# The search's row of norms moved from ScalarE to GpSimd, one tile ahead

## The chip, the cores and the metric

The kernel runs on one core of a Trainium2 chip. A core has five engines that run their own instruction queues in order and meet through semaphores: TensorE (PE in the profile; PEld is its weight load), VectorE (DVE), ScalarE (ACT), GpSimd (POOL) and SyncE (SP), which here only issues transfers. Matmul results lie in PSUM, everything else on chip in SBUF, and 16 DMA engines move data to and from HBM. The metric is the device time of one execution in microseconds (us); smaller is better.

## The reference

Sixteen images of 64 x 64 tokens with 256 channels, float32, pass through four residual layers. Each layer takes a group norm of its input and adds its result to it:

```python
def encode(x, embeddings):                      # layer 0
    xf = x.reshape(-1, x.shape[-1])
    dis = sum(xf*xf, -1) + sum(embeddings*embeddings, 0) - 2.0 * matmul(xf, embeddings)
    return argmin(dis, -1)
x = x + take(embeddings.T, encode(_gn(x), embeddings))   # 1024 codes
x = x + sigmoid(f g^T) h                        # layer 1: attention along each image row of 64
x = x + sigmoid(x2 . softmax(x0 x1^T)) * gn     # layer 2: 4096 x 4096 softmax from three rows, a gate
x = x + layernorm(linear_attention(gn))         # layer 3: 4 heads of 32
```

The change lies in layer 0, the search for the nearest of 1024 codes for each of 65,536 tokens. Beside it, layer 2 matters: for every image it takes the exponential of a 4096 x 4096 outer product and two sums over it.

## The kernel before

The work of an image is cut into stages, each a Python generator: `stats0` (statistics for the first norm), `stage1` (the search), `layer1`, `rows2` and `stage2` (the softmax), `gate2`, and `stage3`. A list of tasks gives every stage of every image a start and a length in units of one image's turn, and a heap takes the generators' steps in the order of those times (L914 to L944). So, in the steady state, VectorE's queue holds, side by side, the search of image b, layer 1 of image b-1, the exponentials of another image, and so on. A scheduler then puts the instructions into one fixed order per engine, and gives them their buffers; at run time each queue is strictly in order.

**The search, `stage1`.** The tokens come in 8 chunks of 4 tiles of 128 tokens. Per image it is 32 tiles, for 16 images 512. For a chunk, `norm` (L329) makes the normed tokens `xn` and their squares `sq` on ScalarE, TensorE sums the squares with a weight of -1 (`px`, L341), ScalarE copies the row (L346), TensorE turns it (`pxt`, L348), and `norm_rows` (L350) copies it on VectorE into `nx2`, four columns of minus the token's squared norm (L353). `ne2`, made once at the start, holds minus the squared norms of the 1024 codes in every partition. For each tile:

- ScalarE makes `nn` = `ne2` + the tile's column of `nx2` (L382), a 128x1024 float32 tile.
- TensorE makes `pd`, twice the products of tokens and codes, in four matmuls (L387).
- VectorE adds `pd` and `nn` into `nn` and takes the largest element (L393), then finds its index (L398).
- GpSimd gathers the 128 rows of the code book by that index and adds them to the tokens `xc`, with an indirect DMA (L399).

`nn` lies in the buffers with tag `t4`, three in number, which `sq`, layer 1's `fg` (L470) and the rows of layer 2 (L578) use too. When a chunk has gone through, `back` (L358) turns the tokens again on TensorE and stores them for layer 1.

**The exponentials, `stage2`.** Per image 64 steps, 1024 in all: ScalarE makes `ex` from the row `x0b` (L627, 128x2048, with the sum as a by-product), and VectorE multiplies `ex` by the row `x2b` and sums it (L630). Both inputs of L630 lie in SBUF. So do those of `gate2`'s L685.

**What else GpSimd does.** In layer 3, `normalize` multiplies the queries by the inverse of their sums (L738), L784 subtracts their maximum; both are `tensor_tensor` instructions on 128x512 in place. L850 takes a power of 4 columns, L280 and L282 finish a group norm, and L611 reduces over the partitions, for which GpSimd's code is exchanged and put back afterwards.

Of the kernel before, what the change touches and what calls it, by code (L numbers as in the profile page):

```python
# [9 lines left out]
F32 = mybir.dt.float32  # L10
BF16 = mybir.dt.bfloat16
U32 = mybir.dt.uint32
AF = mybir.ActivationFunctionType
ALU = mybir.AluOpType
AX = mybir.AxisListType

P = 128
# [4 lines left out]
CH = 4  # L22
# [5 lines left out]
CODES = 1024  # L28
# [13 lines left out]
def kernel(  # L42
# [7 lines left out]
    nc = tc.nc  # L50
# [8 lines left out]
    s1p = ctx.enter_context(tc.tile_pool(name="s1p", bufs=2))  # L59
# [8 lines left out]
    def bank(name):  # L68
        return ps_m.tile([P, 512], F32, tag="pm", name=name)

    def wide(name):
        return ps_w.tile([P, 1024], F32, tag="pw", name=name)
# [113 lines left out]
    ne2 = const.tile([P, CODES], F32, name="ne2")  # L186
# [60 lines left out]
    for n in range(4):  # L247
        t = const.tile([P, 8], F32, name=f"m8_{n}")
# [4 lines left out]
    def stats_tile(kind, name):  # L253
        return small.tile([P, NK, NCHUNK, 6], F32, tag=f"gn_st{kind}", name=name, bufs=1)

    def chunk_stats(st, xt, ch):
        for k in range(NK):
            nc.vector.bn_stats(st[:, k, ch, :], xt[:, k, :])
# [54 lines left out]
    def stage1(b):  # L313
        tag = f"s1_{b}"
        scale, _, nbias = norm0.pop(b)
        src = xT[b].rearrange("(k p) n -> p k n", p=P)
        tok = x[b].rearrange("(t p) c -> p t c", p=P)
        xt, xc, xn, nx2, pxt = {}, {}, {}, {}, {}

        def load(ch):  # L320
            xt[ch] = xa.tile([P, NK, CW], F32, tag="xa", name=f"xt_{tag}_{ch}")
            nc.sync.dma_start(out=xt[ch], in_=src[:, :, ch * CW : (ch + 1) * CW])

        def tokens(ch):
            xc[ch] = s1p.tile([P, CH, C], F32, tag="xc", name=f"xc_{tag}_{ch}")
            nc.sync.dma_start(out=xc[ch], in_=tok[:, ch * CH : (ch + 1) * CH, :])

        def norm(ch):
            xn[ch] = s1p.tile([P, NK, CW], F32, tag="xn", name=f"xn_{tag}_{ch}")  # L329
            sq = s1p.tile([P, NK, CW], F32, tag="t4", name=f"sq_{tag}_{ch}", bufs=3)  # L330
            for k in range(NK):
                nc.scalar.activation(  # L332
                    xn[ch][:, k, :], xt[ch][:, k, :], AF.Identity, bias=nbias[:, k : k + 1], scale=scale[:, k : k + 1]
                )
                nc.scalar.activation(
                    sq[:, k, :], xt[ch][:, k, :], AF.Square, bias=nbias[:, k : k + 1], scale=scale[:, k : k + 1]
                )
            px = bank(f"px_{tag}_{ch}")
            for t in range(CH):
                for k in range(NK):  # L340
                    nc.tensor.matmul(  # L341
                        px[32 * t : 32 * t + 32, :P], lhsT=neg32, rhs=sq[:, k, t * P : (t + 1) * P],
                        start=(k == 0), stop=(k == NK - 1),
                    )
            xrow = small.tile([P, P], F32, tag="xrow", name=f"xrow_{tag}_{ch}", bufs=1)
            nc.scalar.copy(xrow, px[:, :P])  # L346
            pxt[ch] = bank(f"pxt_{tag}_{ch}")
            nc.tensor.transpose(pxt[ch][:, :P], xrow, ident)  # L348

        def norm_rows(ch):  # L350
            px = pxt.pop(ch)
            nx2[ch] = small.tile([P, CH], F32, tag="x2", name=f"nx2_{tag}_{ch}")
            nc.vector.tensor_copy(nx2[ch], px[:, :P].rearrange("p (t n) -> p t n", n=32)[:, :, 0])  # L353

        st1 = stats_tile(1, f"st1_{tag}")
        x1_d[b] = []

        def back(ch):  # L358
            for k in range(NK):
                pt = bank(f"pt_{tag}_{ch}_{k}")  # L360
                for t in range(CH):
                    nc.tensor.transpose(  # L362
                        pt[:, t * P : (t + 1) * P], xc[ch][:, t, k * P : (k + 1) * P], ident
                    )
                nc.scalar.copy(xt[ch][:, k, :], pt)
            chunk_stats(st1, xt[ch], ch)
            d = dram.tile([P, NK, CW], F32, tag=f"x1_{ch}", name=f"x1_{tag}_{ch}")
            nc.scalar.dma_start(out=d, in_=xt.pop(ch))
            x1_d[b].append(d)

        load(0)
        load(1)
        norm(0)
        norm_rows(0)
        tokens(0)
        yield 4
        for ch in range(NCHUNK):
            for t in range(CH):
                T = ch * CH + t

                nn = s1p.tile([P, CODES], F32, tag="t4", name=f"nn_{tag}_{T}", bufs=3)
                nc.scalar.activation(nn, ne2, AF.Identity, bias=nx2[ch][:, t : t + 1])  # L382
                pd = wide(f"pd_{tag}_{T}")
                for hf in range(2):
                    cols = slice(hf * 512, (hf + 1) * 512)
                    for k in range(NK):
                        nc.tensor.matmul(  # L387
                            pd[:, cols], lhsT=xn[ch][:, k, t * P : (t + 1) * P], rhs=e2[:, k, cols],
                            start=(k == 0), stop=(k == NK - 1),
                        )  # L390

                m8 = m8s[T % 4]
                nc.vector.tensor_tensor_reduce(  # L393
                    out=nn, in0=pd, in1=nn, scale=1.0, scalar=-3.0e38, op0=ALU.add, op1=ALU.max,
                    accum_out=m8[:, 0:1],
                )
                i8 = small.tile([P, 8], U32, tag="i8", name=f"i8_{tag}_{T}", bufs=4)
                nc.vector.max_index(i8, m8, nn)  # L398
                nc.gpsimd.indirect_dma_start(  # L399
                    out=xc[ch][:, t, :], out_offset=None,  # L400
                    in_=emb_rows, in_offset=bass.IndirectOffsetOnAxis(ap=i8[:, 0:1], axis=0),
                    compute_op=ALU.add,
                )
                yield 4
                if t == 1 and ch > 0:
                    back(ch - 1)
                    yield 2
                if t == 2 and ch + 1 < NCHUNK:
                    norm(ch + 1)
                    yield 2  # L410
                if t == 3:
                    if ch + 1 < NCHUNK:
                        norm_rows(ch + 1)
                        tokens(ch + 1)
                    if ch + 2 < NCHUNK:
                        load(ch + 2)
        back(NCHUNK - 1)
        with tc.high_priority(offset=URGENT):
            norm1[b] = gn_finish(st1, "n1", b)
        yield 3  # L420
# [518 lines left out]
    while queue:  # L939
        now, n = heapq.heappop(queue)  # L940
        _, length, gen, total = tasks[n]
# [39 lines left out]
```

## Time and profile before

| | |
|---|---|
| timed executions | 5732.52, 5749.94, 5752.01 us; median 5749.94 |
| profiled execution, span from first to last instruction | 5743.5 us (the page gives no other time for it) |
| granted TensorE clock, mean | 0.953 |
| busy: PE / DVE / ACT / POOL | 5264.6 / 5074.3 / 4498.8 / 1721.5 us |
| the same from 1000 to 5000 us | 3777.0 / 3718.6 / 3306.1 / 1270.9 us of 4000 |

Busy time is the union of an engine's instructions; PE's ends are modelled, so its share is an upper view. A group is named by line, engine, operation, tile written <- tiles read; in the names all digits are left out, so `nn_s` is `nn` of the search, `ex_s` the exponentials, `ne` is `ne2`. The idle time beside a group is put down to the instruction whose semaphore came last.

The first image's search runs alone from 40.8 us, the first L630 starts at 320 us, the last search tile's index is looked for at 5056 us and the last L630 starts at 5584 us.

### The profile page before, as it was taken

How to read it: one execution, taken by the hardware profiler on the slowest of the kernel's cores; microseconds unless marked ns; L12 is line 12 of the kernel's file. 1: busy time of each engine (PE TensorE's matmuls, PEld its weight loads, DVE VectorE, ACT ScalarE, POOL GpSimd, SP SyncE). 2: the span in 40 equal slices, each digit the busy share in tenths (PEclk: the TensorE clock that was granted, in tenths of full speed). 3: DMA queues.
4: the chain of work that ended last, by engine and by line, in shares of the span. 5: the costliest groups of instructions: out<-in, count | busy, mean ns of one | idle time of the engine just before them, and what ended most of it. 6: DMA issues, size and time to landing. Idle time of an engine off the chain costs nothing.

```text
span 5743.5 us, 80122 instructions
## 1 busy us (share of the span) xinstructions
PE 5264.6 (92%) x28975; PEld 3227.5 (56%) x28975; DVE 5074.3 (88%) x7186; ACT 4498.8 (78%) x6514; POOL 1721.5 (30%) x1074
## 2 busy tenths in 40 slices
PE   8978899889999999999999999999999999997888
PEld 3534455545656556565655656565565655664556
DVE  6489799999989999998999999999999999998882
ACT  4478588878878788887978788787888879887873
POOL 3123233223333232322323232332323233311221
PEclk9988999989999999999999999999999999998888
DMA  6453836655665656566475656746566674745543
GB/s 184 133 165 93 263 111 196 198 156 170 212 192 174 228 157 217 168 201 223 149 248 158 216 181 198 233 149 223 174 210 194 188 229 151 227 157 180 198 159 116
DMA packets 521380, 1059.52 MB, mean 184 GB/s; under 512 B 52504, under 2 KB 266392, under 8 KB 512792
## 3 DMA queue, kind: packets, MB, share of 16 engines
q1 hardware_dynamic: 406288, 885.11, 45.5%
q0 software_dynamic: 73728, 67.14, 8.2%
q10 hardware_dynamic: 40968, 102.13, 4.6%
q8 instruction: 230, 3.77, 0.3%
q14 instruction: 166, 1.36, 0.1%
HBM read 751.18 MB, written 303.04 MB: 184 GB/s over the span
## 4 chain that ended last, share of the span: by engine, by line
PE 40%; DVE 16%; ACT 11%; issue 4%; DMA 4%; POOL 4%; SPq 0%; ACTq 0%; POOLq 0%; DVEq 0%
PE pd_s L387 12%; DVE ex_s L630 6%; ACT ex_s L627 5%; PE ph_l L477 3%; PE pxo_s L890 3%; PE pqv_s L764 2%; PE pk_s L747 2%; PE po_l L515 2%; DMA qo_s<-qd_s 2%; PE pxo_s L884 2%; PE pz_s L839 2%; POOL qv_s L784 2%; DVE i_s L398 2%; DVE nn_s L393 1%; PE pvr_s L847 1%
## 5 line engine op out<-in xcount | busy, mean ns | idle before, releaser
L630 DVE CUSTOM_DVE_ANT_0 ex_s<-ex_s,x2b 128x2048 f32<-128x2048 f32 x1024 | 2398.0, 2349 | 65.9 <-ACT ex_s L627 65.8
L627 ACT ACTIVATE ex_s<-x0b,nmax_s,x_r 128x2048 f32<-128x2048 f32 x1024 | 2138.1, 2089 | 42.9 <-DVE num_s L630 34.3
L387 PE MATMUL pd_s<-e,xn_s 128*128 128x512 f32 x4096 | 1989.0, 620 | 44.9 <-DVE m L393 33.6
L399 POOL DMA_INDIRECT xc_s<-in_emb_rows,i_s x512 | 1091.3, 2131 | 1926.7 <-DVE i_s L398 1406.6
L387 PEld LDWEIGHTS pd_s<-e,xn_s 128*128 128x128 f32 x4096 | 752.8, 196 | 810.3 <-issue 697.6
L393 DVE CUSTOM_DVE_ANT_0 nn_s<-pd_s,nn_s 128x1024 f32<-128x1024 f32 x512 | 620.2, 1213 | 157.9 <-PE pd_s L387 87.4
L398 DVE FIND_INDEX8 i_s<-m,nn_s 128x8 uint32<-128x1024 f32 x512 | 623.4, 1218 | 0.0
L382 ACT ACTIVATE nn_s<-ne,nx_s 128x1024 f32<-128x1024 f32 x512 | 582.6, 1144 | 45.2 <-DVE nx_s L353 21.5
L477 PE MATMUL ph_l<-wh_l,xt_l 128*128 128x256 f32 x2048 | 525.5, 393 | 20.8 <-DVE m L393 12.1
L764 PE MATMUL pqv_s<-wqv_s,xk_s 128*128 128x256 f32 x2048 | 488.9, 380 | 0.0
L477 PEld LDWEIGHTS ph_l<-wh_l,xt_l 128*128 128x128 f32 x2048 | 382.3, 194 | 135.9 <-issue 64.1
L764 PEld LDWEIGHTS pqv_s<-wqv_s,xk_s 128*128 128x128 f32 x2048 | 388.8, 191 | 119.9 <-issue 60.2
L784 POOL TENSOR_TENSOR qv_s<-qv_s,qm_s 128x512 f32<-128x512 f32 x128 | 195.3, 1526 | 679.9 <-DVE qm_s L783 492.7
L850 POOL TENSOR_TENSOR lrs_s<-lrs_s,mhalf 128x4 f32<-128x4 f32 x128 | 163.6, 1278 | 678.0 <-ACT lrs_s L849 664.2
L515 PEld LDWEIGHTS po_l<-at_l,h_l 64*128 64x128 f32 x4096 | 260.6, 193 | 61.3 <-issue 29.1
L515 PE MATMUL po_l<-at_l,h_l 64*128 64x64 f32 x4096 | 288.7, 283 | 4.5 <-DVE m L393 2.9
L738 POOL TENSOR_TENSOR qv_s<-qv_s,qd_s 128x512 f32<-128x512 f32 x128 | 203.6, 1590 | 266.5 <-DVE qd_s L737 101.4
L890 PE MATMUL pxo_s<-wctx_s,qo_s 128*128 128x256 f32 x1024 | 272.8, 390 | 0.8 <-DVE qo_s L858 0.8
L895 ACT COPY y_s<-pxo_s 128x512 f32<-128x512 f32 x256 | 149.0, 582 | 153.7 <-PE pxo_s L894 131.7
L747 PE MATMUL pk_s<-xk_s,wk_s 128*128 128x512 f32 x512 | 256.6, 624 | 1.5 <-DMA xk_s<-x_g 1.5
L362 PE MATMUL pt_s<-ident,xc_s 128*128 128x128 f32 x1024 | 161.1, 287 | 101.5 <-DMA xc_s<-in_emb_rows,i_s 71.7
L332 ACT ACTIVATE xn_s<-xt_s,nb_n,s_n 128x512 f32<-128x512 f32 x256 | 200.9, 807 | 50.5 <-PE pd_s L387 28.4
(201 smaller groups left out, 7306.4 us busy)
## 6 DMA issues: line engine op xcount, KB each, us to landing
xs_s<-in_xT SPq DMA_DIRECT2D x128, 512.0 KB
xt_s<-in_xT SPq DMA_DIRECT2D x128, 512.0 KB
xc_s<-in_x SPq DMA_DIRECT2D x128, 512.0 KB
x_s<-xt_s ACTq DMA_DIRECT2D x128, 512.0 KB
xt_l<-x_s SPq DMA_DIRECT2D x128, 512.0 KB
x_l<-xt_l SPq DMA_DIRECT2D x128, 512.0 KB
xr_r<-x_l SPq DMA_DIRECT2D x128, 512.0 KB
xg_g<-x_l SPq DMA_DIRECT2D x128, 512.0 KB
```

The source lines that it names most:

```text
L382: nc.scalar.activation(nn, ne2, AF.Identity, bias=nx2[ch][:, t : t + 1])
L387: nc.tensor.matmul(pd[:, cols], lhsT=xn[ch][:, k, t * P : (t + 1) * P], rhs=e2[:, k, cols], start=(k == 0), stop=(k == NK - 1),)
L393: nc.vector.tensor_tensor_reduce(out=nn, in0=pd, in1=nn, scale=1.0, scalar=-3.0e38, op0=ALU.add, op1=ALU.max, accum_out=m8[:, 0:1],)
L398: nc.vector.max_index(i8, m8, nn)
L399: nc.gpsimd.indirect_dma_start(out=xc[ch][:, t, :], out_offset=None, in_=emb_rows, in_offset=bass.IndirectOffsetOnAxis(ap=i8[:, 0:1], axis=0),
L477: nc.tensor.matmul(ph[:, t, :], lhsT=X[:, k, t * P : (t + 1) * P], rhs=wh_n[:, k, :], start=(t % 2 == 0 and k == 0), stop=False, skip_grou ...
L515: nc.tensor.matmul(po[:, r, k * CH + t, :], lhsT=h[rows, t, k * P : (k + 1) * P], rhs=at[rows, t, :], start=True, stop=True,)
L627: nc.scalar.activation(ex, x0b, AF.Exp, bias=nmax[:, T : T + 1], scale=x01[:, T, 1:2], accum_out=den[:, h, T : T + 1])
L630: nc.vector.tensor_tensor_reduce(out=ex, in0=ex, in1=x2b, scale=1.0, scalar=0.0, op0=ALU.mult, op1=ALU.add, accum_out=num[:, h, T : T + 1],)
L747: nc.tensor.matmul(pk, lhsT=wk_n[:, k, :], rhs=xt[:, k, :], start=(k == 0), stop=(k == NK - 1))
L764: nc.tensor.matmul(pqv[:, j, :], lhsT=xt[:, k, t * P : (t + 1) * P], rhs=wqv_n[:, k, :], start=(j == 0 and k == 0), stop=False, skip_group ...
L890: nc.tensor.matmul(px[:, j, :], lhsT=qT[:, t * P : (t + 1) * P], rhs=wctx[:, 1, :], start=False, stop=False, skip_group_check=True,)
```

## The change

A function `base` makes `nn` with a `tensor_scalar` on GpSimd: `ne2` x 1.0 + the column of `nx2`. It is called one tile ahead: for the first tile of a chunk where `norm_rows` is called, for the others at the head of the step of the tile before. In program order it so stands in front of the gather of the tile before. The activation L382 on ScalarE goes. The buffers stay three.

```diff
+        sums = {}
+
+        def base(ch, t):
+            T = ch * CH + t
+            sums[T] = s1p.tile([P, CODES], F32, tag="t4", name=f"nn_{tag}_{T}", bufs=3)
+            nc.gpsimd.tensor_scalar(sums[T], ne2, 1.0, nx2[ch][:, t : t + 1], ALU.mult, ALU.add)
+
         load(0)
         load(1)
         norm(0)
         norm_rows(0)
         tokens(0)
+        base(0, 0)
         yield 4
         for ch in range(NCHUNK):
             for t in range(CH):
                 T = ch * CH + t
 
-                nn = s1p.tile([P, CODES], F32, tag="t4", name=f"nn_{tag}_{T}", bufs=3)
-                nc.scalar.activation(nn, ne2, AF.Identity, bias=nx2[ch][:, t : t + 1])
+                if t + 1 < CH:
+                    base(ch, t + 1)
+                nn = sums.pop(T)
                 pd = wide(f"pd_{tag}_{T}")
...
                     if ch + 1 < NCHUNK:
                         norm_rows(ch + 1)
                         tokens(ch + 1)
+                        base(ch + 1, 0)
                     if ch + 2 < NCHUNK:
                         load(ch + 2)
```

## The prediction

> **What bounds the kernel now.** I read the page first for the engines' shares and the chain, then the groups by line, VectorE's waits, the table by stages, and last the timeline at the places where GpSimd and VectorE run together.
>
> ```profile
> PE 5264.6 (92%) x28975; PEld 3227.5 (56%) x28975; DVE 5074.3 (88%) x7186; ACT 4498.8 (78%) x6514; POOL 1721.5 (30%) x1074
> ...
> PE 40%; DVE 16%; ACT 11%; issue 4%; DMA 4%; POOL 4%; SPq 0%; ACTq 0%; POOLq 0%; DVEq 0%
> ...
> L630 DVE CUSTOM_DVE_ANT_0 ex_s<-ex_s,x2b 128x2048 f32<-128x2048 f32 x1024 | 2398.0, 2349 | 65.9 <-ACT ex_s L627 65.8
> ...
> L382 ACT ACTIVATE nn_s<-ne,nx_s 128x1024 f32<-128x1024 f32 x512 | 582.6, 1144 | 45.2 <-DVE nx_s L353 21.5
> ```
>
> No engine waits much: the chain passes through all of them, and TensorE and VectorE lead. By stages it is clearer:
>
> ```profile
> 1000.00:5000.00 4000.00, 3776.96 (x21279) 2325.21 (x21278) 3718.56 (x5217) 3306.10 (x4769) 1270.94 (x768) 0.97 0.61 193
> ```
>
> After window and length the columns are PE, PEld, DVE, ACT and POOL. In the 4000 us in which all stages run together VectorE is busy 93% and idle for 281 us; ScalarE, which the change relieves, is at 83%. So time added to VectorE has little room, and time taken from ScalarE counts only where something waits for ScalarE. VectorE's longest waits:
>
> ```profile
> DVE nn_s L393 <- PE pd_s L387: 87.4, 52, 12.4
> DVE qz_s L841 <- PE pz_s L839: 71.1, 40, 4.2
> DVE ex_s L630 <- ACT ex_s L627: 65.8, 65, 2.9
> DVE nn_s L393 <- ACT nn_s L382: 50.3, 43, 3.9
> ```
>
> The wait for the moved instruction itself is 50.3 us. Summed over the whole list, waits that ScalarE ends make 242 us of VectorE's 669 us idle, waits that TensorE ends 345 us.
>
> The timeline shows what GpSimd can do to VectorE (start, length, engine and line):
>
> ```profile
> 2029.98 4.46 DVE L630 CUSTOM_DVE_ANT_0 ex_s<-ex_s,x2b 128x2048 f32<-128x2048 f32 x1
> ...
> 2037.02 2.27 DVE L630 CUSTOM_DVE_ANT_0 ex_s<-ex_s,x2b 128x2048 f32<-128x2048 f32 x1
> ```
>
> ```profile
> 2029.64 1.55 POOL L399 DMA_INDIRECT xc_s<-in_emb_rows,i_s  x1 [1.37 <-DVE qd_s L737]
> 2030.61 1.67 POOL L738 TENSOR_TENSOR qv_s<-qv_s,qd_s 128x512 f32<-128x512 f32 x1
> ```
>
> The same L630 takes 2.27 us alone and 4.46 us here: it ends 2.16 us after GpSimd's L738 has ended at 2032.28, as if it had begun only then. L738 stood behind a gather with its input ready, and VectorE was shut out for the gather and L738 together. The other order exists too:
>
> ```profile
> 2082.30 2.28 DVE L630 CUSTOM_DVE_ANT_0 ex_s<-ex_s,x2b 128x2048 f32<-128x2048 f32 x1
> ...
> 2084.84 2.80 DVE L630 CUSTOM_DVE_ANT_0 ex_s<-ex_s,x2b 128x2048 f32<-128x2048 f32 x1
> ```
>
> ```profile
> 2082.63 2.86 POOL L784 TENSOR_TENSOR qv_s<-qv_s,qm_s 128x512 f32<-128x512 f32 x1
> ```
>
> Here L630 was first, GpSimd's L784 (median 1.05 us) took 2.86 us, and the next L630 paid 0.52 us. So an L630 and a GpSimd `tensor_tensor` never run together; who comes first blocks the other. Gathers alone don't do this: of 332 L630 that overlap nothing but gathers none is over 2.30 us.
>
> ```profile
> L630 DVE CUSTOM_DVE_ANT_0 ex_s<-ex_s,x2b x1024: 2220/2281/4461, 320.2 to 5583.8; 128x2048 f32<-128x2048 f32 x171
> ```
>
> The median is 2.281 us, so L630's 2398.0 us hold 2398.0 - 1024 x 2.281 = 62 us of blocking, by 256 `tensor_tensor` (L738 and L784): 0.24 us each.
>
> **The change, part by part.**
>
> *Taken from ScalarE:* 512 x 1.144 = 583 us. ScalarE falls from 4499 to 3916 us. On the path this is worth at most the 242 us of waits that ScalarE ends, and at least nothing; the rest of ScalarE's chain (L627 before L630, the copies out of PSUM) keeps its own lengths and only gets its turn earlier. I take half, -121 us.
>
> *Put on GpSimd:* 512 `tensor_scalar` of 128x1024, one input. The trace of before has no such row. L784 reads two inputs of 512, also 1024 elements per partition, in 1.05 us: lower end. By L784's rate per element written, (1.05 - 0.19) / 512 with 0.19 us for the 128x2 row of L282, 1024 would take 0.19 + 1.72 = 1.9 us: upper end. I take 1.2 us, near the first, since reading two inputs is what makes L784 dear. GpSimd then has 1722 + 614 = 2336 us, 41%: it isn't the bound.
>
> [...]
>
> *VectorE blocked.* The new instruction reads SBUF, as L738 and L784 do. In the build's order for GpSimd 226 of the 512 stand directly behind a gather, 206 behind another of their own, 80 behind something else; 276 carry no wait at all, so they're ready while the gather in front still runs, as L738 was above. I laid them into the trace of before in that order: each asks for the port when its buffer is free (the search three tiles back has ended) and the instruction in front has begun, gets it then or when a running L630 or L685 ends, and keeps it until its own end. Counting the L630 and L685 that start inside such a stretch: at 1.06 us 200 of them lose 278 us, at 1.2 us 217 lose 324 us, at 1.9 us 267 lose 614 us. The low end is the rate of the existing ones, 512 x 0.24 = 123 us; if one input instead of two lets VectorE pass, it is nothing. I take 324 us.
>
> [...]
>
> *How much of the 324 us shows.* While VectorE is held, TensorE works ahead, so waits that TensorE ends shrink. They can't shrink by more than their 345 us, nor below none; I take a third, -115 us. Check in the middle stage: it has 378 of the 512 tiles, so 239 us are added to 3719, together 3958 of 4000. VectorE would be at 99% if nothing got longer; at 97% the stage takes 4080 us, +80.
>
> *VectorE's wait for `nn`.* In the same count 43 tiles get `nn` late, by 52 us together, against the 50.3 us now: nothing. If GpSimd takes 1.9 us it is 94 us.
>
> *What queues behind.* GpSimd is in order. Behind a new instruction that waits for its buffer (177 name TensorE, 127 VectorE) or the port stand gathers (+0.3 us each in the count), L784 (+1.4), L738 (+0.9) and the power L850 (+0.2). Gathers are needed only by `back`, six tiles or so later; TensorE waits 72 us for them now. L784 holds ScalarE's L785, which waits 153 us for it already, and L738 TensorE's L726 (25 us). Of 180 + 121 us added I take a tenth on the chain, +30 us; ends 0 and +300.
>
> *Buffers.* `nn` is held a tile longer in three buffers that `sq` shares: 95 of 256 `sq` now wait for VectorE instead of 55. ScalarE loses 12.4 us so today; 12.4 x 95/55 is 21, +9 us on an engine that has just been freed: nothing on the path, and 9 us without that cover. The order of VectorE's queue hardly changes (each L393 stays within 8 L630 of its place), and TensorE's and SyncE's keep their instructions.
>
> Sum against the profiled span: 5743.5 - 121 + 324 - 115 + 30 = 5861.5. The median lies 6.4 us above the span: 5868 us, 2.1% slower.
>
> **The rivals.**
>
> 1. *VectorE passes* (faster). A one-input GpSimd instruction might not shut L630 out; every row that shows it has two inputs. Then 5743.5 - 121 + 30 + 6.4 = 5659 us. For it: the 128x4 power L850 and gathers overlap L630 without cost. Against it: they read next to nothing. It decides the sign once the loss per new instruction is under some 0.18 us, that is (121 - 30) / 512.
> 2. *A draw.* The loss stays at today's 0.24 us each, 123 us, and VectorE's order hides the queueing: 5743.5 - 121 + 123 + 6.4 = 5752 us. For it: ready instructions may go in L393 or L398, 2.4 us per tile that need only one SBUF input. Against it: the gather in front comes at L398's end, just when VectorE turns to the next instruction.
> 3. *GpSimd becomes the wait* (slower still). At 1.9 us the count gives 614 us, and L784 and L738 wait 221 and 134 us; with 60 us of them on the chain 5743.5 - 121 + 614 - 115 + 60 + 6.4 = 6188 us. For it: the unknown duration. Against it: one input.
>
> **How the numbers follow.** My forecast has 0.60 (its own range 5790 to 6010), VectorE passes 0.13, a draw 0.10, GpSimd the wait 0.17. This kernel's three runs spread over 0.34%, so 0.5% is about what tells from no change. Predicted is the likeliest, 5868. The range has to reach the draw and most of the third rival: 5725 to 6190 leaves out rival 1 and the upper part of rival 3, about 0.19. Faster has rival 1 and a little of the draw, 0.14; within 0.5% most of the draw and a little of the forecast's low end, 0.10; slower the rest, 0.76.
>
> **What the profile after would show.** L382's group gone, ACT near 3916 us; a POOL group of 512 at 1.05 to 1.9 us where VectorE leaves it alone, with a tail above 3 us; L630's mean up from 2.349 to about 2.65 us with hundreds above 2.4 us (72 now), most of them beside a new instruction; DVE busy near 5390 us and over 95% from 1000 to 5000 us; L393's waits for GpSimd near 50 us. I'm wrong if L630 keeps its mean (rival 1), if L630 stretches but the span doesn't (the slack was larger than its 281 us in the middle), or if L393 waits hundreds of us for GpSimd.

## The result, and the profile after

The changed kernel takes 6001.53 us (median; 5992.86 to 6019.43) against 5741.23 us for the kernel before on the same chip: ratio 1.0453, 95% interval 1.0427 to 1.0479. It is 260 us, 4.5%, slower; the forecast was 5868 us. The profiled execution is the slowest of the four; its span is 6017.7 us, 274.2 us above the 5743.5 us of before. Below, the lines of the code have moved: L382 is now L376 on GpSimd, L393 is L402, L398 is L407, L399 is L408, L627 is L637, L630 is L640, L685 is L695, and L738 and L784 are L748 and L794.

The page's engine line, the chain's shares and the groups that answer to those shown of before:

```profile
PE 5345.5 (89%) x28975; PEld 3253.7 (54%) x28975; DVE 5247.9 (87%) x7186; ACT 3996.7 (66%) x6002; POOL 2516.6 (42%) x1586
...
PE 36%; DVE 30%; issue 12%; POOL 9%; ACT 7%; DMA 6%; SPq 0%; POOLq 0%; ACTq 0%; DVEq 0%
...
L640 DVE CUSTOM_DVE_ANT_0 ex_s<-ex_s,x2b 128x2048 f32<-128x2048 f32 x1024 | 2509.4, 2457 | 67.1 <-ACT ex_s L637 67.0
L637 ACT ACTIVATE ex_s<-x0b,nmax_s,x_r 128x2048 f32<-128x2048 f32 x1024 | 2140.7, 2091 | 278.6 <-DVE num_s L640 264.1
...
L376 POOL TENSOR_SCALAR nn_s<-ne,nx_s 128x1024 f32<-128x1024 f32 x512 | 828.5, 1705 | 300.9 <-DVE nx_s L353 144.1
L402 DVE CUSTOM_DVE_ANT_0 nn_s<-pd_s,nn_s 128x1024 f32<-128x1024 f32 x512 | 620.6, 1213 | 264.8 <-POOL nn_s L376 131.5
```

ScalarE lost its 512 activations, and it now stands idle 264.1 us in front of the exponentials, waiting for VectorE to give their buffer back. In the kernel before that wait was

```profile
ACT ex_s L627 <- DVE num_s L630: 34.3, 33, 4.7
```

What ScalarE gave up came back as waiting. VectorE's exponentials L640 take 2509.4 us instead of 2398.0, and the new row of GpSimd takes 1.705 us on average. In the table by stages, with the columns as before:

```profile
1000.00:5000.00 4000.00, 3643.44 (x19907) 2216.84 (x19906) 3635.41 (x4938) 2751.97 (x4117) 1763.56 (x1085) 0.95 0.59 184
```

VectorE does less in these 4000 us than before (3635 instead of 3719), though each exponential takes longer. So the slowdown has two halves, and the span can be split exactly by VectorE's books: 5247.9 - 5074.3 = 174 us more of busy time and (6017.7 - 5247.9) - (5743.5 - 5074.3) = 101 us more of idle time. The busy half first (start, length, engine, line, from the timeline of the kernel after):

```profile
2520.09 2.28 DVE L640 CUSTOM_DVE_ANT_0 ex_s<-ex_s,x2b 128x2048 f32<-128x2048 f32 x1
...
2520.45 3.39 POOL L408 DMA_INDIRECT xc_s<-in_emb_rows,i_s  x1 [0.90 <-DVE i_s L407]
...
2522.89 4.28 DVE L640 CUSTOM_DVE_ANT_0 ex_s<-ex_s,x2b 128x2048 f32<-128x2048 f32 x1
...
2523.28 1.74 POOL L376 TENSOR_SCALAR nn_s<-ne,nx_s 128x1024 f32<-128x1024 f32 x1
```

The second L640 takes 4.28 us: it ends 2.15 us after the new instruction's end at 2525.02, as if it had begun only then. The new instruction has one input and still holds VectorE up, as L738 did in the trace of before. That is what I call the lock, and what the forecast calls the port: of the 237 overlaps of a new instruction with an L640, L640 ends at least 2.13 us after the instruction in 129 and the instruction at least 0.98 us after L640 in 108, nearly their whole lengths alone (2.22 and 1.108 us at least), so the two never ran together. By what means, no run shows. Over the whole trace 334 L640 that overlap nothing of GpSimd and 268 that overlap gathers only never take more than 2.294 us; of 108 that overlap only the new instruction 66 are stretched, up to 3.161 us. I call "stretch" what VectorE's instructions take beyond the median of their operation and shape, where that is more than 0.1 us: 84 us before, 251 us after, 222 of these in L640 and L695. Of the 251 us, 181 lie in instructions that overlap a new one.

The idle half is in VectorE's waits:

```profile
DVE nn_s L402 <- POOL nn_s L376: 131.5, 84, 2.9
DVE nn_s L402 <- PE pd_s L396: 120.0, 64, 12.4
```

Before, `nn` cost 50.3 us and `pd` 87.4 us. Of the 84 waits for `nn` nearly all, 79 with 127.1 us, fall on the first tile of a chunk, whose `nn` is ready at the median 0.03 us ahead of L402; the other three tiles of the chunk have it 5.5, 15.4 and 19.9 us ahead. Over all its lines VectorE waits 182 us for GpSimd (45 before), 379 us for TensorE (345) and 172 us for ScalarE (242).

### The profile page after: what moved, and what is told of

The parts are those of the page before. It is cut to its first block, busy times and chain, and to the rows that moved or that the text cites. A ratio compares the mean times of both kernels' runs of the same rounds, so it can differ in the third digit from the quotient of the medians.

```text
span 6017.7 us, 80376 instructions
## 1 busy us (share of the span) xinstructions
PE 5345.5 (89%) x28975; PEld 3253.7 (54%) x28975; DVE 5247.9 (87%) x7186; ACT 3996.7 (66%) x6002; POOL 2516.6 (42%) x1586
## 4 chain that ended last, share of the span: by engine, by line
PE 36%; DVE 30%; issue 12%; POOL 9%; ACT 7%; DMA 6%; SPq 0%; POOLq 0%; ACTq 0%; DVEq 0%
DVE ex_s L640 11%; PE pd_s L396 11%; DVE i_s L407 5%; POOL nn_s L376 4%; PE ph_l L487 4%; ACT ex_s L637 3%; DVE nn_s L402 3%; PE pxo_s L900 2%; PE po_l L525 2%; POOL xc_s L408 2%; PE pqv_s L774 2%; DVE xg_g L695 2%; DVE st_s L258 2%; PE pz_s L849 2%; PE pk_s L757 1%
## 5 line engine op out<-in xcount | busy, mean ns | idle before, releaser
L640 DVE CUSTOM_DVE_ANT_0 ex_s<-ex_s,x2b 128x2048 f32<-128x2048 f32 x1024 | 2509.4, 2457 | 67.1 <-ACT ex_s L637 67.0
L637 ACT ACTIVATE ex_s<-x0b,nmax_s,x_r 128x2048 f32<-128x2048 f32 x1024 | 2140.7, 2091 | 278.6 <-DVE num_s L640 264.1
L396 PE MATMUL pd_s<-e,xn_s 128*128 128x512 f32 x4096 | 2046.4, 634 | 108.4 <-DVE m L402 98.1
L408 POOL DMA_INDIRECT xc_s<-in_emb_rows,i_s x512 | 1119.0, 2186 | 1584.6 <-DVE i_s L407 1287.3
L396 PEld LDWEIGHTS pd_s<-e,xn_s 128*128 128x128 f32 x4096 | 765.5, 201 | 899.4 <-issue 728.9
L376 POOL TENSOR_SCALAR nn_s<-ne,nx_s 128x1024 f32<-128x1024 f32 x512 | 828.5, 1705 | 300.9 <-DVE nx_s L353 144.1
L402 DVE CUSTOM_DVE_ANT_0 nn_s<-pd_s,nn_s 128x1024 f32<-128x1024 f32 x512 | 620.6, 1213 | 264.8 <-POOL nn_s L376 131.5
L407 DVE FIND_INDEX8 i_s<-m,nn_s 128x8 uint32<-128x1024 f32 x512 | 622.3, 1216 | 0.0
L794 POOL TENSOR_TENSOR qv_s<-qv_s,qm_s 128x512 f32<-128x512 f32 x128 | 235.7, 1842 | 383.3 <-DVE qm_s L793 331.1
L860 POOL TENSOR_TENSOR lrs_s<-lrs_s,mhalf 128x4 f32<-128x4 f32 x128 | 180.0, 1406 | 491.7 <-ACT lrs_s L859 485.3
L748 POOL TENSOR_TENSOR qv_s<-qv_s,qd_s 128x512 f32<-128x512 f32 x128 | 208.8, 1632 | 372.2 <-DVE qd_s L747 149.5
L335 ACT ACTIVATE sq_s<-xt_s,nb_n,s_n 128x512 f32<-128x512 f32 x256 | 198.2, 807 | 90.8 <-DVE i_s L407 87.8
```

What stands on the lines that cost most here:

```text
L376: nc.gpsimd.tensor_scalar(sums[T], ne2, 1.0, nx2[ch][:, t : t + 1], ALU.mult, ALU.add)
L396: nc.tensor.matmul(pd[:, cols], lhsT=xn[ch][:, k, t * P : (t + 1) * P], rhs=e2[:, k, cols], start=(k == 0), stop=(k == NK - 1),)
L402: nc.vector.tensor_tensor_reduce(out=nn, in0=pd, in1=nn, scale=1.0, scalar=-3.0e38, op0=ALU.add, op1=ALU.max, accum_out=m8[:, 0:1],)
L408: nc.gpsimd.indirect_dma_start(out=xc[ch][:, t, :], out_offset=None, in_=emb_rows, in_offset=bass.IndirectOffsetOnAxis(ap=i8[:, 0:1], axis=0),
L637: nc.scalar.activation(ex, x0b, AF.Exp, bias=nmax[:, T : T + 1], scale=x01[:, T, 1:2], accum_out=den[:, h, T : T + 1])
L640: nc.vector.tensor_tensor_reduce(out=ex, in0=ex, in1=x2b, scale=1.0, scalar=0.0, op0=ALU.mult, op1=ALU.add, accum_out=num[:, h, T : T + 1],)
```

## The experiments

Theories that stood against each other: the time is VectorE's stretch beside the new instruction (the forecast's own reason); it is the late `nn`; it is that `nn` is held a tile longer in three buffers; it is GpSimd's queue, with the exchange of its code for the reduction over partitions; or it is merely ScalarE's new order.

One thing goes along with every edit below: the scheduler makes a new fixed order for each kernel. Counted in the traces, 3488 of VectorE's 7186 instructions stand at another place of its queue after than before, nine in ten of all within five places; between `relief` and the kernel before it is 3687, between `fill` and the kernel after 1108, between a kernel with three buffers and the same with four 2443 to 2984 (1200 for the kernel before). Between `first` and `firstfill` it is 90, and GpSimd's order is the same: that pair changes one thing nearly alone. No run holds the order fixed for the others, so their prices hold the new order's part. `relief` is as much reordered as the kernel after and `before_b4` a third as much, and their times differ from the kernel before by +0.4% and -0.1%.

### Take the instruction away, or replace it by one that reads nothing

`relief` is the kernel before without the instruction that makes `nn`; VectorE adds `ne2` itself, and the tile `nn` only takes the sum:

```diff
-                nc.scalar.activation(nn, ne2, AF.Identity, bias=nx2[ch][:, t : t + 1])
...
-                    out=nn, in0=pd, in1=nn, scale=1.0, scalar=-3.0e38, op0=ALU.add, op1=ALU.max,
+                    out=nn, in0=pd, in1=ne2, scale=1.0, scalar=-3.0e38, op0=ALU.add, op1=ALU.max,
```

> L382 is dropped and nothing takes its place: VectorE adds the codes' norms alone, the token's norm is left out of the computation. This is ScalarE's relief by itself, without GpSimd. My prediction priced the relief at -121 us (half of the waits that ScalarE ends): about 5620 us. If the relief is worth only the wait for nn itself (50 us) it gives about 5690 us; if ScalarE has slack enough everywhere, 5740 us as before.

Measured: 5758.11 us, ratio 1.0039 (1.0020 to 1.0058). ScalarE is relieved of all its 512 activations, GpSimd has got nothing, and the kernel is no faster. VectorE's busy time fell by 26 us and its idle time rose by 60 us: its waits for ScalarE fell from 242 to 195 us, those for TensorE rose from 345 to 445 us. Its wait for `pd` rose from 87.4 us and ScalarE's wait for VectorE in front of the exponentials from 34.3 us to these:

```profile
DVE nn_s L392 <- PE pd_s L386: 153.5, 114, 11.5
```

```profile
ACT ex_s L626 <- DVE num_s L629: 153.7, 131, 4.8
```

The term for ScalarE's relief fell here.

`fill` lets GpSimd do about as much, in the same place and the same buffers, but without reading the tile from SBUF:

```diff
-            nc.gpsimd.tensor_scalar(sums[T], ne2, 1.0, nx2[ch][:, t : t + 1], ALU.mult, ALU.add)
+            nc.gpsimd.memset(sums[T], -1.0)
+            nc.gpsimd.tensor_scalar(sums[T][:, 0:1], ne2[:, 0:1], 1.0, nx2[ch][:, t : t + 1], ALU.mult, ALU.add)
```

> As the changed kernel, but GpSimd only writes the 1024 columns (a constant) and adds the norms in one column, so that the instruction that reads SBUF is 1 column long: same place in GpSimd's queue, same buffers and waits; the sum of norms is left out for 1023 columns. Port theory (VectorE's L640 and L695 are held while GpSimd reads SBUF): L640 back near 2.34 us in the mean, DVE busy near 5080 us, the time falls by about 170 us to 5830 or less. Queue theory (the loss is GpSimd's order and the late nn): stays above 5950 us with DVE busy unchanged only if the stretch isn't the cause.

Measured: 5858.15 us, ratio 1.0218 (1.0182 to 1.0254); GpSimd is busy 2563 us against 2517 us in the kernel after, VectorE's stretch is 114 us instead of 251. GpSimd's queue in `fill`'s timeline, and below it the group of its L641, which is L640 of the kernel after:

```profile
3004.89 1.55 POOL L376 MEMSET nn_s<- 128x1024 f32 x1
...
3015.07 1.60 POOL L409 DMA_INDIRECT xc_s<-in_emb_rows,i_s  x1 [0.16 <-DVE num_s L641]
...
3016.09 1.54 POOL L376 MEMSET nn_s<- 128x1024 f32 x1
...
3017.04 1.30 POOL L377 TENSOR_SCALAR nn_s<-ne,nx_s 128x1 f32<-128x1 f32 x3
```

```profile
L641 DVE CUSTOM_DVE_ANT_0 ex_s<-ex_s,x2b 128x2048 f32<-128x2048 f32 x1024 | 2378.7, 2329 | 54.5 <-ACT ex_s L638 54.4
```

GpSimd's queue is filled as in the kernel after, gather, fill and column in a row, but L641's mean is 2.329 us, below the 2.349 us of before. 220 L641 overlap a fill and no `tensor_tensor`, and none of them takes more than 2.293 us; the 44 that are stretched all overlap a `tensor_tensor`. So it is the instruction that reads the tile from SBUF that shuts the exponentials out here (66 of the 108 that overlap it alone are stretched), not one that writes as much (none of the 220) and not GpSimd's being busy. (Some short VectorE instructions with one input do wait for a fill, 32 of them for 37 us together; see the last section.) The reading, with what hangs on it, is worth 6001.53 - 5858.15 = 143 us. The other half, 2.2%, stays, and L403 still waits 110.5 us for `nn`; both theories that give one cause alone are out.

### Move the first tile back, or drop the lead

`first` leaves the first tile of each chunk to ScalarE where it was before; GpSimd makes the other 384 ahead:

```diff
-        base(0, 0)
...
+                if t == 0:
+                    nn = s1p.tile([P, CODES], F32, tag="t4", name=f"nn_{tag}_{T}", bufs=3)
+                    nc.scalar.activation(nn, ne2, AF.Identity, bias=nx2[ch][:, 0:1])
+                else:
+                    nn = sums.pop(T)
...
-                nn = sums.pop(T)
...
-                        base(ch + 1, 0)
```

> As the changed kernel, but the first tile of each chunk (128 of 512) is made by ScalarE in its old place; the other 384 stay on GpSimd one tile ahead. Late-first-tile theory: 127 of the 131 us that VectorE waits for GpSimd's nn fall on the first tile of a chunk, so they fall back to the 35 us of before, and a quarter of the stretch of L640 and L695 goes too: about 5870 us. If only the number of GpSimd instructions matters, a quarter of the 260 us goes: about 5935 us.

Measured: 5906.47 us, ratio 1.0299 (1.0262 to 1.0335), 95 us under the kernel after. That is between the two forecasts. VectorE's waits for `nn` are 5.6 us for GpSimd and 39.7 us for ScalarE instead of 131.5 us. A quarter of the new instructions is gone too, and the stretch is 201 us instead of 251: the run prices the late tile and that quarter together.

`now` puts the GpSimd instruction where the activation stood, with no lead (against the kernel before):

```diff
-                nc.scalar.activation(nn, ne2, AF.Identity, bias=nx2[ch][:, t : t + 1])
+                nc.gpsimd.tensor_scalar(nn, ne2, 1.0, nx2[ch][:, t : t + 1], ALU.mult, ALU.add)
```

> The activation's place is kept, only its engine changes: GpSimd makes nn in the tile's own step, not one tile ahead. If the lead is what keeps the loss down, VectorE waits for nn in all four tiles of a chunk and the time rises above 6050 us. If the lead buys nothing (the first tile of a chunk has none, the others come 6 to 20 us early), it stays within 30 us of the changed kernel, or falls because GpSimd holds the port and the buffers less long at bad moments.

Measured: 5930.92 us, ratio 1.0334 (1.0298 to 1.0370). Without the lead the kernel is 71 us faster than with it: VectorE's wait for GpSimd's `nn` is 90.0 us instead of 131.5. The lead gives the other three tiles time that they don't need, and the first tile can't use it, since its `nx2` column comes from VectorE only just before. `now` doesn't hold `nn` a tile longer either, and TensorE's `px` waits 20.9 us for `sq` instead of 55.7; so part of the 71 us can be the buffers'.

### More and less of the instruction

`twice` issues it a second time, `one` leaves it for the third tile of each chunk alone (128 of 512), the rest on ScalarE:

```diff
             nc.gpsimd.tensor_scalar(sums[T], ne2, 1.0, nx2[ch][:, t : t + 1], ALU.mult, ALU.add)
+            nc.gpsimd.tensor_scalar(sums[T], ne2, 1.0, nx2[ch][:, t : t + 1], ALU.mult, ALU.add)
```

> As the changed kernel, with the tensor_scalar issued twice for every tile (the second writes the same values again). Port theory: another 512 reads of SBUF by GpSimd hold VectorE again for some 0.3 us each, +160 us, and the first tile of each chunk is late by another 1.1 us, +90 us: about 6250 us. If the loss comes from where nn stands in the order and the buffers, and not from what GpSimd does, it stays under 6060 us.

> Only the third tile of each chunk (128 of 512) is made by GpSimd, one tile ahead; ScalarE makes the other 384. If every such instruction costs what the port costs, about 0.3 us, it is 40 us slower than before, 5780 us. If the relief of ScalarE by a quarter were worth something, it would be at 5740 us or below.

Measured: `twice` 6302.35 us, ratio 1.0966 (1.0936 to 1.0997), `one` 5844.55 us, ratio 1.0178 (1.0147 to 1.0209). `twice` adds 301 us to the kernel after, of which only 58 us are VectorE's busy time: GpSimd is late, and L403 (L402 after) waits for it:

```profile
DVE nn_s L403 <- POOL nn_s L377: 276.4, 108, 6.6
```

So GpSimd turns into the wait at twice the work. In `one` nearly everything is lock: VectorE has 89 us more of busy time and 6 us more of idle time than before. 128 instructions cost 87 us of stretch, 0.68 us each, against 167 us or 0.33 us each for the 512 after; counting only what overlaps a new instruction, 0.57 and 0.35 us. Both forecasts for `one` were too low. The instruction is the same in both kernels, so its price isn't set by its length alone; what sets it, what it stands behind or what VectorE runs at that moment, wasn't separated.

### The exchange of GpSimd's code

In the trace after, 32 MODIFY_POOL_CONFIG stand in GpSimd's queue at the 16 reductions and 32 more at the elementwise instructions behind them, 0.65 and 0.63 us at the median; that they exchange GpSimd's code is my reading of them. The elementwise instruction that follows a reduction over the partitions comes 8 to 15 us later than the reduction, though in 14 of the 16 cases a gather starts within 3 us:

```profile
2093.80 0.37 POOL L621 PARTITION_ALL_REDUCE ab_s<-ext_s  x1 [7.37 <-DVE st_g L258]
...
2094.36 1.80 POOL L408 DMA_INDIRECT xc_s<-in_emb_rows,i_s  x1 [0.19 <-issue]
...
2104.67 1.11 POOL L376 TENSOR_SCALAR nn_s<-ne,nx_s 128x1024 f32<-128x1024 f32 x1 [8.51 <-issue]
...
2105.81 1.23 DVE L402 CUSTOM_DVE_ANT_0 nn_s<-pd_s,nn_s 128x1024 f32<-128x1024 f32 x1 [1.02 <-POOL nn_s L376]
```

`noswap_after` and `noswap_before` make that reduction (16 of them) on TensorE and VectorE, so there is nothing to exchange GpSimd's code for, in the kernel after and in the kernel before:

```diff
-        nc.gpsimd.partition_all_reduce(ab, ext, P, bass_isa.ReduceOp.max)
+        pe_ = bank(f"pext_{tag}")
+        nc.tensor.transpose(pe_[:2, :P], ext, ident)
+        emax = small.tile([2, 1], F32, tag="emax", name=f"emax_{tag}", bufs=1)
+        nc.vector.tensor_reduce(emax, pe_[:2, :P], AX.X, ALU.max)
+        ed = small.tile([2, 2], F32, tag="ed", name=f"ed_{tag}", bufs=1)
+        nc.vector.tensor_scalar(ed, ident[0:2, 0:2], emax, None, ALU.mult)
+        pa = bank(f"pab_{tag}")
+        nc.tensor.matmul(pa[:, 0:2], lhsT=one[0:2, :].to_broadcast([2, P]), rhs=ed, start=True, stop=True)
+        nc.vector.tensor_copy(ab, pa[:, 0:2])
```

> As the changed kernel, but L621's reduction over the partitions, for which GpSimd's code is exchanged twice per image, is done by TensorE and VectorE. In the changed kernel GpSimd can't make nn for some 17 us around each reduction. Code-exchange theory: these 16 stretches cost VectorE 3 to 8 us each, so the time falls by 50 to 130 us, to 5870 to 5950 us. If nn is late only because it has no lead at the head of a chunk, it falls by under 20 us, and as much as the same edit gives the kernel before.

> The same edit of the reduction in the kernel before, where nn is ScalarE's: the control. VectorE idles 107 us in the 16 windows of 30 us around the reduction, some 50 us more than its average share. If those come from the exchange of code (L784 and the power L850 wait for it), the time falls to about 5700 us; if from the chain of layer 2's start itself, it stays at 5738 us or rises by the few us of the added steps.

Measured: `noswap_after` 5966.89 us, ratio 1.0401 (1.0369 to 1.0433); `noswap_before` 5765.15 us, ratio 1.0044 (1.0027 to 1.0061). The kernel after gains 0.5% where the kernel before loses 0.4%, so the exchange takes part in the slowdown with something like 35 to 58 us (the larger if the other way to reduce costs the same 0.4% in both). It is not the main cause.

### The buffers

`b4` gives `t4` four buffers, and makes room by cutting `v2`, which layer 3 uses, from seven to five; `v5` is the kernel before with that cut alone:

```diff
-            sq = s1p.tile([P, NK, CW], F32, tag="t4", name=f"sq_{tag}_{ch}", bufs=3)
+            sq = s1p.tile([P, NK, CW], F32, tag="t4", name=f"sq_{tag}_{ch}", bufs=4)
...
-            qT = s3p.tile([P, CW], F32, tag="v2", name=f"qT_{tag}_{ch}", bufs=7)
+            qT = s3p.tile([P, CW], F32, tag="v2", name=f"qT_{tag}_{ch}", bufs=5)
```

(and so at every other tile with these two tags)

> As the changed kernel, with four buffers of tag t4 instead of three; layer 3's tag v2 has five instead of seven to make the room. Buffer theory: nn made ahead holds two of three buffers, so sq waits for VectorE (88 us in the changed kernel, 12 before), the norms of the next chunk are late, and with them the first nn: a fourth buffer gives back 50 to 100 us, about 5920 us. If the buffers don't matter it stays near 6000 us, or rises by what the two buffers of layer 3 cost.

> The control for the run with four buffers: the kernel before with five buffers of layer 3's tag v2 instead of seven. If the two buffers matter little, 5740 us within 0.5%, and the 75 us that the fourth t4 buffer gave back are its own. If it is slower, the fourth buffer is worth that much more; if it is faster, so much less.

Measured: `b4` 5926.94 us, ratio 1.0320 (1.0289 to 1.0352), 75 us under the kernel after; `v5` 5737.40 us, ratio 0.9989 (0.9972 to 1.0006), so the cut costs nothing. Three buffers aren't free, then. But VectorE's books don't show the path that the theory named. The page of `b4`:

```profile
PE 5304.0 (90%) x28975; PEld 3247.8 (55%) x28975; DVE 5151.3 (87%) x7186; ACT 3992.9 (67%) x6002; POOL 2583.5 (44%) x1586
```

Of a span of 5918.8 us VectorE is idle 767.5 us, as in the kernel after (769.8); what fell is its stretch, from 251 to 158 us. `sq` waits 69.5 us instead of 87.8 and `pd` costs 79.0 us instead of 120.0, but other waits grew as much. Why a fourth buffer shortens the stretch is open. `firstfill` combines `first` and `fill`, which takes away the late first tile and the lock of the exponentials together:

> Both causes taken away at once: the first tile of a chunk on ScalarE as in the run with 384 tiles on GpSimd, and those 384 made by writing a constant and one column, so that GpSimd hardly reads SBUF (the norms of 1023 columns are left out for them). If port and late first tile are all there is, it ends within 1% of the kernel before, 5740 to 5790 us. If GpSimd's queue and the buffers cost something of their own, it stays above 5800 us.

Measured: 5833.71 us, ratio 1.0149 (1.0116 to 1.0182). Stretch is 88 us and VectorE waits 17 us for GpSimd's `nn` (its fill and its column), yet 1.5% stays, most of it as 77 us of VectorE's idle time. Its waits suggest the path:

```profile
DVE nn_s L406 <- PE pd_s L400: 141.8, 99, 11.4
...
PE px_s L341 <- ACT sq_s L335: 67.2, 52, 4.7
...
ACT sq_s L335 <- DVE i_s L411: 55.7, 32, 5.0
```

The last two in the kernel before:

```profile
PE px_s L341 <- ACT sq_s L335: 20.8, 27, 2.2
...
ACT sq_s L335 <- DVE i_s L398: 12.4, 8, 2.4
```

ScalarE's `sq` waits for a buffer until VectorE has finished an earlier tile's search, TensorE's `px` waits for `sq`, and `pd`, behind `px` in TensorE's queue, comes late. These lines alone don't prove it: in `relief`, where no tile is held longer, `sq` waits 6.5 us for VectorE and `pd` still costs 153.5 us. `firstfill_b4` is the same with four `t4` buffers:

> firstfill (tile 0 of a chunk on ScalarE, the other 384 as a fill of 128x1024 and a 1-column tensor_scalar on GpSimd) with four t4 buffers instead of three, and five v2 buffers instead of seven to make room. As in firstfill, the sum of the norms is left out in 1023 columns of the 384 tiles. firstfill stood 1.5% (about 90 us) over before although its stretch (88 us against 84) and VectorE's wait for a late nn were both gone. Theory, three buffers: nn held one tile longer makes sq wait for VectorE and px for sq, and pd comes late; with a fourth buffer the waits of sq and px fall back to before's 12 and 21 us and the time goes to 5740 to 5775 us, ratio 1.000 to 1.005. Rival, GpSimd's queue and the order: the gathers, the two tensor_tensor and the reduction over partitions stand behind 384 instructions more, and ScalarE's work falls out of step; then the time stays at 5810 to 5850 us, ratio 1.012 to 1.018, whatever the buffers.

Measured: 5711.33 us, ratio 0.9949 (0.9925 to 0.9972), and the same three waits:

```profile
DVE nn_s L406 <- PE pd_s L400: 107.8, 76, 11.5
...
ACT sq_s L335 <- DVE i_s L411: 37.8, 21, 5.1
...
PE px_s L341 <- ACT sq_s L335: 13.2, 24, 2.4
```

The time is below the range that the theory gave; `px` waits less than before, `sq` still three times as long. One buffer, with the order that comes with it, is worth 122 us here, 92 of the profile's 124 us as less idle time. With the lock, the late tile and the buffer gone, nothing of the slowdown is left. What GpSimd's 384 x 2 more instructions cost and what ScalarE's relief brings stand in this figure together. The last two runs ask whether the fourth buffer would help the kernel before as well, and what the whole computation costs with both mends that leave it whole:

> The kernel before with four t4 buffers instead of three, and five v2 buffers instead of seven to make room: the control for the fourth buffer without the change. In before sq waits 12 us for VectorE and px 21 us for sq. If the fourth buffer only gives back what the change took (nn held a tile longer), it does little here: ratio 0.998 to 1.002. If three buffers are a limit of before too, the gain of firstfill_b4 against before (0.995) is the buffer's alone and shows here: ratio 0.990 to 0.997. If it is ScalarE's relief that shows once the lock, the late nn and the buffers are out of the way, this run stays within 0.2% of before.

> The whole computation with the mends that the runs gave: tile 0 of each chunk on ScalarE in its old place, tiles 1 to 3 by the tensor_scalar on GpSimd ahead, four t4 buffers, five v2 buffers. Against firstfill_b4 it differs only in what GpSimd runs: the tensor_scalar, which reads 128x1024 of SBUF, instead of the fill, which reads none. If late nn, buffers and the port lock are the three costs, the first two are gone and the lock stays: VectorE is stretched by 100 to 170 us and the time is 5790 to 5860 us, ratio 1.009 to 1.021. If the buffers were the whole cost and the lock hides in VectorE's slack, it comes to 5700 to 5750 us, ratio 0.993 to 1.002. If the costs don't add up, it stays near first, 5880 to 5910 us.

Measured: `before_b4` 5727.92 us, ratio 0.9993 (0.9977 to 1.0010); `first_b4` 5805.61 us, ratio 1.0122 (1.0100 to 1.0143). So the fourth buffer does nothing without the change: it is the change that needs it. And `first_b4` against `firstfill_b4`, which differ in whether GpSimd reads the tile and in the place of 391 of VectorE's instructions, shows the lock nearly by itself, 94 us; `first` against `firstfill`, with 90 displaced, gives 73 us. Its exponentials beside those of `firstfill_b4`, first one kernel, then the other:

```profile
L642 DVE CUSTOM_DVE_ANT_0 ex_s<-ex_s,x2b 128x2048 f32<-128x2048 f32 x1024 | 2464.1, 2414 | 45.0 <-ACT ex_s L639 43.5 <-issue 1.2
```

```profile
L643 DVE CUSTOM_DVE_ANT_0 ex_s<-ex_s,x2b 128x2048 f32<-128x2048 f32 x1024 | 2344.4, 2297 | 43.9 <-ACT ex_s L640 43.5
```

### The sum

Ratios to the kernel before:

| what makes `nn` | 3 buffers | 4 buffers |
|---|---|---|
| GpSimd, all 512 tiles, reads the tile (the change) | 1.0453 | 1.0320 |
| GpSimd, 384 tiles, reads the tile; ScalarE the chunks' first | 1.0299 | 1.0122 |
| GpSimd, 384 tiles, only fills; ScalarE the chunks' first | 1.0149 | 0.9949 |
| ScalarE, all (the kernel before) | 1 | 0.9993 |

Down the columns the first tile's move, with a quarter of the locking instructions in it, costs 1.5 and 2.0%, the lock of 384 instructions 1.5 and 1.7%. Across, three buffers instead of four cost 1.3, 1.8 and 2.0%, and 0.1% (not told from nothing) without the change. With all three mended 0.9949 is left against 0.9993, about 25 us: ScalarE's relief of 384 activations, less what GpSimd's fuller queue costs. The three costs of some 1.5 to 2% each less 0.4% make the 4.5% along this way through the table; by another way each has another size. In every row the order and TensorE's granted clock (0.940 to 0.958 in the profiles of these eight kernels) changed along.

No run here beats the kernel before with the whole computation done; `before_b4` is level with it.

## Why the prediction was right or wrong

The direction was right, and the result lies in its range, but the likeliest figure fell short by 133 us, 2.1% instead of 4.5%, and the terms behind it were wrong in both directions. The steps that failed are a gain that didn't come (ScalarE's relief, -121 us) and two costs put at nothing (the late `nn`, the held buffer), which the runs price at 1.5 to 2.0% and 1.3 to 2.0%. The stretch, put twice too large, covered a part of what was left out: that the result still lies in the range is luck in so far.

**ScalarE's relief, -121 us: wrong.** `relief` takes the whole 583 us off ScalarE and comes out 0.4% slower; at best, in `firstfill_b4`, three quarters of it are worth some 25 us. "At least nothing" was the end to take. The step that failed is to book half of the waits that ScalarE ends as gain. In `relief` 47 of these 242 us did go, but VectorE's waits for TensorE grew by 100 us. And when ScalarE has less to do it reaches the next exponential earlier and waits there for VectorE to free the buffer (34.3 us before, 153.7 in `relief`, 264.1 after).

**VectorE blocked, +324 us: right in kind, twice too large.** One input locks like two: 66 of the 108 L640 that overlap the new instruction alone are stretched, up to 3.161 us, as before 47 of the 101 L630 that overlap L738 or L784 alone, up to 3.137 us. The instruction's length was right (1.108 us at least, 1.2 us taken), though L784, from which it came, is no row of two full inputs: its second is 16 values, each used 32 times. Why that row takes 1.05 us for 512 elements written, no run shows. But the stretch rose from 84 to 251 us, 167 us, or 0.33 us for each instruction instead of 0.63; in L640 and L695, which alone the count took, it is 140 us. 164 L640 are stretched where 72 were, and not two hundred more. The step that failed is the count, which laid instructions into the times of the old trace, while in the new one GpSimd is late itself and half of VectorE's instructions stand elsewhere. Which rule of the count failed wasn't separated.

**Less waiting for TensorE, -115 us: the share was right, the rest wrong.** I let about two thirds of the stretch show. Between `firstfill_b4` and `first_b4` the stretch rises by 193 - 64 = 129 us and the time by 94 us, between `firstfill` and `first` by 113 and 73 us: 73 and 65%. But waits for TensorE shrink by only 11 and 22 us in these pairs, and in the kernel after itself they grew, from 345 to 379 us. A fourth buffer takes them back to 346 us.

**VectorE's wait for `nn`, nothing: wrong.** The count gave 43 late tiles and 52 us; the trace has 84 waits and 131.5 us, and moving the first tile back is worth 95 us (the lock of 128 instructions in it). I looked at the tiles together, and a lead of one tile looks safe for the mean. The chunk's first tile has no lead at all: its input comes from L353 immediately before, where ScalarE needed 1.14 us at once and GpSimd's record lasts 1.71 us at the median, with gathers in front of it. With the fill in place of the read, moving that tile back saves only 24 us by the medians and 0.7% by the ratios (`fill` to `firstfill`): much of the 95 us hangs on the lock, and the terms don't simply add.

**What queues behind GpSimd, +30 us: not shown.** The two runs without the exchange of code put 35 to 58 us on that, which I hadn't named at all, so a like size is luck. In `firstfill_b4`, which keeps the exchange and has a full queue, nothing of the slowdown is left; so the queue's cost, if there is one, is no larger there than what ScalarE's relief brings.

**Buffers, nothing: the largest miss.** I saw that 95 of 256 `sq` would wait, priced the wait at 9 us of ScalarE, which I took to be free, and stopped there. The wait was 75 us longer (12.4 to 87.8), and the engine that pays isn't ScalarE. A fourth buffer is worth 75 to 122 us, none of it without the change. In `firstfill` it goes the way of `sq`, `px` and `pd` to VectorE's idle time; in the kernel after itself it shows as VectorE's stretch, by a way that stays open. What is late next wasn't asked of this wait. I also wrote that VectorE's order hardly changes: L402 does keep its place among the L640 (within 4), but half of VectorE's instructions moved.

Of the rivals, "VectorE passes" and "a draw" are out by the stretch and by the time. "GpSimd becomes the wait" came nearer than it looked: L402's longest wait is for GpSimd, 131.5 us, and `twice` is that rival (276.4 us). Of the signs to look for, VectorE's 5390 us and 95% in the middle were not there (5248 us, 91%): its idle time grew, where the forecast had it shrink.

## What to carry to other kernels

An engine with the least busy time isn't a free place (here GpSimd, 30% busy, at a cost of 4.5%): ask of a moved instruction what it reads and which instructions it runs beside, which one of its tiles has no lead, and which buffer it now holds longer, and follow each to the engine that pays last. The time taken off a busy engine is worth nothing until a run with the work simply left out shows a gain; here that run came out at +0.4%. When one cost is mended, measure the others again beside it, since here the same buffer was worth 1.3, 1.8 and 2.0% as the other costs went away.

## What the runs showed of the hardware

- GpSimd's `tensor_scalar`, which reads one 128x1024 tile from SBUF, stretches the exponentials, which read two SBUF tiles: of 108 L640 that overlap it alone 66 are stretched, up to 3.161 us, where L640 takes 2.280 us at the median with nothing of GpSimd beside it. GpSimd filling a tile of the same size (0.941 us at least, against 1.108 us) doesn't stretch a single one of 220 exponentials. L402, which reads `pd` from PSUM and one SBUF tile, and L407, which reads one, aren't stretched: of 108 and 58 that overlap the new instruction alone none takes more than 1.226 and 1.221 us, against 1.214 us at the median for both with nothing of GpSimd beside them.
- Beside a fill some other VectorE instructions are stretched. In `fill`

```profile
3402.80 1.61 POOL L409 DMA_INDIRECT xc_s<-in_emb_rows,i_s  x1 [0.35 <-DVE ext_s L619]
3403.82 1.56 POOL L376 MEMSET nn_s<- 128x1024 f32 x1
```

```profile
3403.81 1.61 DVE L655 TENSOR_SCALAR gate_s<-gate_s 128x32 f32<-128x32 f32 x1
```

  a one-input `tensor_scalar` of 128x32, 0.18 us at the median in the kernel before (L644), takes 1.61 us and ends 0.04 us after the fill. 32 VectorE instructions that overlap fills but no 128x512 `tensor_tensor` are stretched there, by 37 us together, 13 of them this one.
- The lock works in the other direction too. In the timeline of the kernel after

```profile
2003.12 2.63 DVE L640 CUSTOM_DVE_ANT_0 ex_s<-ex_s,x2b 128x2048 f32<-128x2048 f32 x1
...
2003.61 3.13 POOL L376 TENSOR_SCALAR nn_s<-ne,nx_s 128x1024 f32<-128x1024 f32 x1
```

  GpSimd's instruction starts 0.49 us after L640 and ends at 2006.74, 0.99 us after L640's end at 2005.75; it is one of the 108 overlaps of that trace in which GpSimd's instruction ends last. Gathers are longer there too: in the kernel before, the 163 that start while an L630 runs take 3.36 us at the median, the other 349 take 1.57 us.
- After a reduction over the partitions GpSimd starts a gather within 0.2 to 2.7 us (14 of 16 cases in the kernel after) but its next elementwise instruction only 8 to 15 us later.
- TensorE's mean granted clock was 0.953 before, 0.942 after, 0.943 in `firstfill` and 0.958 in `firstfill_b4`, and the products' matmul took 620, 634, 626 and 622 ns. How much of the idle time is this clock's doing, and how much the clock follows from the waits, no run here separates.
